# Graph attention over 16 batches: the loads of a batch moved between its four slots, and x in three buffers instead of four

## The chip, the cores and the metric

One core of one Trainium2 chip. The metric is device time in microseconds, the median of several runs; one more execution was recorded by the profiler. The core's engines are TensorE (PE; its weight loads are listed apart as PEld), VectorE (DVE), ScalarE (ACT), GpSimd (POOL) and SyncE (SP). In this kernel SP computes nothing: it issues nearly all DMAs.

## What is computed

A graph attention layer over 16 batches of 512 nodes with 512 features. Each node attends to the first 20 nodes (the "keys"), with 16 heads of 32 features, in two directions (d = 0, 1), each with its own weights and its own view of the adjacency mask. All is 32-bit float. Cut to the core:

```python
row_zero  = v.sum(-1) == 0
q_exp     = where(row_zero[..., None], 0, q[:, None, :])
self_feat = concat([v, q_exp], -1) @ W_self.T + b_self
output    = self_feat
for d in range(2):
    A   = (adj if d == 0 else swapaxes(adj, 1, 2))[:, :, :20, :]     # 11 labels
    kv  = self_feat[:, :20]
    qh, kh = heads(self_feat @ Wq[d].T + bq[d]), heads(kv @ Wk[d].T + bk[d])
    aff = einsum('bnhd,bmhd->bnhm', qh, kh) / sqrt(32)
    aff = where(A.sum(-1) > 0, aff, -9e15) + (A @ w_bias + b_bias)
    w   = softmax(aff, -1)
    output += einsum('bnhf,hgf->bnhg', einsum('bnhm,bmf->bnhf', w, kv), Wout[d]) + bout[d]
return v + relu(output)
```

## The kernel before

Features lie on the partitions (four chunks of 128), nodes along the free dimension. A setup stage (to about 97 us in the profile) makes, for all batches at once, what depends only on the 20 key nodes: the keys already multiplied by the query weights (DRAM buffers `g_d` and `g1_d`), bias scores (`cq_d`), and the values multiplied by the output weights (`vw_d`, later arranged into blocks in `bd_d`). Then a loop runs over the batches b = 0 to 15, and inside it over four tiles `nt` = 0 to 3 of 128 nodes. One pass of the inner loop is called a slot here.

The order is written by hand: `tc.manual_schedule()` keeps each engine's instructions in the order of the program text. What one engine runs is thus fixed, and only semaphores decide when. All loads and stores of the loop are issued by SP, in program order; when one must wait (for its buffer, or for its data), all that stand behind it wait too.

What TensorE does in batch b, in its order:

- slot 0: half of the self features of this batch (`self_feat(b, 0, 1)`, L186, 64 matmuls), then the scores of tile 0 (L250, 128 matmuls);
- slot 1: `self_feat(b, 1, 1)` (64), scores of tile 1 (128);
- slot 2: `attend(b - 1)` (L321: weights times value blocks, for the batch before), scores of tile 2;
- slot 3: the other half of the self features of the next batch (`self_feat(b + 1, 0, 0)` and `(b + 1, 1, 0)`, L186, 128 matmuls), scores of tile 3.

A batch needs these transfers:

| Name | What | Size | First read by |
|---|---|---|---|
| `x` (`load_x`, L88) | node features, features on the partitions | 1024 KB | L186 on TensorE in slot 3 of the batch before; last by `residual` (L335) on GpSimd, in slot 3 of the batch after |
| `xn` (`load_xn`, L92), two halves | the same features, nodes on the partitions | 2 x 512 KB | `row_sum` (L149) on ScalarE, in slot 0 of the batch before |
| `nz` (`load_nz`, L156) | flags of zero rows, written by `row_mask` (L154) in slot 1 | 256 KB | `self_copy` (L199) on VectorE, slot 3 of the batch before |
| `g` (`load_keys`, L110) | keys | 1216 KB | scores (L250) of slot 0 |
| `adj` (`load_adj`, L96), two halves | masks | 2 x 440 KB | `mask_mul` (L207) on ScalarE and `mask_count` (L213) on VectorE: half 0 in slot 2 of the batch before, half 1 in slot 0 |
| `cq` (`load_cq`, L102) | bias scores | 4 x 20 KB | `full_add` (L239) on GpSimd |
| `vd` (`load_values`, L115) | value blocks | 4 x 32 KB | `attend` (L321) in slot 2 of the batch after |
| `out` (`store`, L340) | result of the batch before, four chunks | 4 x 256 KB | stores: two in slot 3, two in the next slot 0, after `residual` (L335) |

In batch 0, `clear_blocks` (L125) zeroes `bd_d` in slot 1, and `blocks` (L142) fills it in slot 2 by 12 DMAs, which wait for the zeroing.

Buffers come from rotating pools: `x` has four, `adj` three, `xn`, `nz`, `cq` and `g` two, `vd` one. A load waits until the last reader of the tile that had its buffer is done. The setup uses one of the x buffers for a weight (`ws_q`). Scores go to PSUM through two buffers (`ps_s`), self features through four (`ps_acc`).

Of the kernel before, what the change touches and what calls it, by code (L numbers as in the profile page):

```python
# [7 lines left out]
F32 = mybir.dt.float32  # L8
# [5 lines left out]
P = 128  # L14
# [4 lines left out]
def gat_kernel(  # L19
# [21 lines left out]
    B, F, N = xT.shape  # L41
    NG, L = adj.shape[3], adj.shape[4]
    H, DH = 16, 32
    C = F // P
# [14 lines left out]
    load = ctx.enter_context(tc.tile_pool(name="load", bufs=2))  # L59
# [24 lines left out]
    xs, xns, rss, adjs, nzs, sfs, cqs, gs, vds = {}, {}, {}, {}, {}, {}, {}, {}, {}  # L84
# [1 line left out]


    def load_x(b):  # L88
        xs[b] = load.tile([P, C, N], F32, tag="x", name=f"x{b}", bufs=4)
        nc.sync.dma_start(xs[b], xT[b].rearrange("(c p) n -> p c n", p=P))  # L90

    def load_xn(b, h):  # L92
        t = xns[b, h] = load.tile([P, 2, F], F32, tag="xn", name=f"xn{b}_{h}")
        nc.sync.dma_start(t, xn[b].rearrange("(p j) f -> p j f", j=4)[:, 2 * h : 2 * h + 2])

    def load_adj(b, h):  # L96
        t = adjs[b, h] = load.tile([P, 2, S * L], I32, tag="adj", name=f"adj{b}_{h}", bufs=3)
        nc.sync.dma_start(
            t, adj[b, h * 2 * P : (h + 1) * 2 * P].rearrange("(t p) d m l -> p t (d m l)", p=P)
        )  # L100

    def load_cq(b):  # L102
        cqs[b] = load.tile([P, HL, S], F32, tag="cq", name=f"cq{b}")
        for a in range(HL):
            nc.sync.dma_start(
                cqs[b][bass.ts(a, R)].rearrange("p h m -> p (h m)"),
                cq_d[b : b + 1, bass.ts(a, HL)].rearrange("b h d m -> b (h d m)").partition_broadcast(R),
            )

    def load_keys(b):  # L110
        gs[b] = gp.tile([P, C, WD], F32, tag="g", name=f"g{b}")
        src = g1_d if b == 1 else g_d[:, :, b - 2]
        nc.sync.dma_start(gs[b].rearrange("p c (a w) -> p (c a) w", a=C), src.rearrange("x p w -> p x w"))

    def load_values(b):  # L115

        vds[b] = gp.tile([P, HL, 2, DH], F32, tag="vd", name=f"vd{b}", bufs=1)
        for c in range(C):
            nc.sync.dma_start(
                vds[b][bass.ts(c, 32)].rearrange("p e i g -> p (e i g)"), bd_d[c, b].rearrange("r e i g -> r (e i g)")  # L120
            )

    def clear_blocks(zero):

        nc.sync.dma_start(  # L125
            bd_d.rearrange("c b r e i g -> (c b r) (e i g)").rearrange("(n p) w -> p n w", p=P),
            zero.unsqueeze(1).to_broadcast([P, C * B * 32 // P, HL * 2 * DH]),
        )

    def blocks():  # L130

        bb = bd_d.rearrange("c b r e i g -> (c b) r e i g")
        vv = vw_d.rearrange("d c (b m) (e g) -> d (c b) m e g", m=NG, e=HL)
        for e in range(HL):
            for i in range(2):
                j = (e * S) // 32 + i
                for d in range(2):
                    lo = max(e * S + d * NG, 32 * j)
                    hi = min(e * S + (d + 1) * NG, 32 * j + 32)
                    if lo < hi:  # L140
                        m, r = lo - e * S - d * NG, lo - 32 * j
                        nc.sync.dma_start(bb[:, r : r + hi - lo, e, i], vv[d, :, m : m + hi - lo, e])  # L142
# [13 lines left out]
    def load_nz(b, queue=nc.sync):  # L156
        nzs[b] = load.tile([P, N], F32, tag="nz", name=f"nz{b}")
        queue.dma_start(nzs[b], nz_d[b : b + 1].partition_broadcast(P))
# [179 lines left out]
    def store():  # L338
        for b, c, o in outs:
            nc.sync.dma_start(out[b, bass.ts(c, P)], o[:, c])  # L340
        outs.clear()


    with tc.tile_pool(name="setup", bufs=1) as sp:
# [12 lines left out]
        ones = sp.tile([P, P], F32, name="ones")  # L357
        br_sb = sp.tile([P, F], F32, name="br_sb")

        ws_q = load.tile([P, C, F], F32, tag="x", name="ws_q", bufs=4)  # L360
        wk_sb = [sfp.tile([P, C, F], F32, tag="sf", name=f"wk{d}") for d in range(2)]

        with tc.tile_pool(name="setup_k", bufs=1) as sk:
# [38 lines left out]
            for d in range(2):  # L402
                rows(wq_sb[:, d], wq[d])
            nc.sync.dma_start(br_sb, b_row.partition_broadcast(P))
            load_x(0)
            nc.sync.dma_start(wb_sb, w_bias.partition_broadcast(P))
            load_adj(0, 0)
# [3 lines left out]
            for d in range(2):  # L411
                rows(wo_sb[:, d], woT[d])
            load_x(1)
            load_adj(0, 1)

# [86 lines left out]
        with tc.tile_pool(name="setup_g", bufs=4) as sg:  # L502
# [116 lines left out]
            for n, runs in enumerate(bursts):  # L619
# [9 lines left out]
                for kind in plan[n - first] if n - first < len(plan) else ():  # L629
                    f, args = steps[kind].pop(0)  # L630
# [25 lines left out]
    with tc.manual_schedule():  # L656
# [11 lines left out]
        for b in range(B):  # L668
# [12 lines left out]
                )  # L681
            for nt in range(NT):
                store()
                if nt == 1:
                    if b + 1 < B:
                        load_adj(b + 1, 0)
                        load_cq(b + 1)
                    if b == 0:
                        clear_blocks(zero)
                if nt == 2:  # L690
                    if b + 1 in rss and b > 0:
                        load_nz(b + 1)
                    if 0 < b < B - 1:
                        load_keys(b + 1)
                    if b == 0:
                        load_adj(1, 1)
                    if b + 2 < B:
                        load_x(b + 2)
                    if 0 < b < B - 1:
                        load_adj(b + 1, 1)  # L700
                    if b + 2 < B:
                        load_xn(b + 2, 0)
                        load_xn(b + 2, 1)
                    if b == 0:
                        blocks()
                if nt == (3 if b + 1 < B else 2):
                    load_values(b)

                if b == B - 1 and nt == 2:
# [85 lines left out]
        b = B - 1  # L795
# [80 lines left out]
```

## Time and profile before

| | |
|---|---|
| Median of 3 runs | 625.6 us (624.79 to 625.65) |
| Profiled execution | 623.73 us, of which the span of the instructions is 621.9 us |
| Granted TensorE clock | 0.995 of full speed |
| DMA traffic | 124.17 MB, mean 200 GB/s; queue q1 (that of SP) 57.5% of the 16 engines' time |
| L250 scores on PE | 285.6 us busy, 8192 matmuls of 293 ns (pipelined) |
| L186 self features on PE | 228.7 us busy, 4096 matmuls of 371 ns (pipelined) |
| PEld waits put down to "issue" | L250 20.6 us (29 times), L186 7.0 us (15 times) |
| DMA issue to landing, median | g 8.7, x 11.0, xn 9.2, adj 7.9, out 3.8, nz 4.4, cq 3.6, vd 5.7 us |

The profile page gives busy time per engine, the queues' traffic, and the chain of work that ended last. Matmuls are pipelined, so the mean of one is longer than the distance between two. "issue" stands for time in which an engine waited for nothing that the profile shows. Besides the page the trace answers questions about stretches of time: the busy time of each engine in a stretch, the DMA engines' share and their rate, and the instructions in order of time, with the idle time before each in square brackets and what ended it. In that timeline a row of SP is the issue of a DMA, not its transfer.

### The profile page before, as it was taken

The page shows a single profiled execution, that of the slowest core. Times are in us where ns is not written, and L with a number is a line of the kernel's source. Part 1 is how long each engine was busy: PE and PEld are TensorE (multiplying, and loading weights), DVE is VectorE, ACT ScalarE, POOL GpSimd, SP SyncE. Part 2 cuts the span into 40 slices and gives each one's busy share as a digit, 9 for nine tenths or more (in the row PEclk, how much of TensorE's full clock was granted, in tenths as well). Part 3 has the DMA queues.
Part 4 walks back from the last instruction along what each step waited for, and adds up shares of the span by engine and source line. Part 5 has one row for each costly group of instructions (what it writes and reads, how often), then busy time and mean ns, then how long its engine had stood idle before and what let it go on. Part 6 is the DMA issues. An engine that isn't in the chain of part 4 may idle for free.

```text
span 621.9 us, 30998 instructions
## 1 busy us (share of the span) xinstructions
PE 607.3 (98%) x13932; PEld 468.4 (75%) x13932; DVE 478.3 (77%) x754; ACT 312.0 (50%) x862; POOL 374.1 (60%) x303
## 2 busy tenths in 40 slices
PE   9999999999999999999999999999999999999995
PEld 6654558787888878878787877878788877787883
DVE  1585657788787878797868788787868797878786
ACT  1334624464555546463637474655546463647561
POOL 3307343557575756666674848475756666675875
PEclk9999999999999999999999999999999999999997
DMA  8999999719282646546381909182735556382503
GB/s 319 385 405 305 356 360 351 181 48 318 60 282 95 223 156 186 192 131 247 93 285 26 332 32 315 56 287 91 243 134 178 201 137 241 79 299 43 167 13 136
DMA packets 97684, 124.17 MB, mean 200 GB/s; under 512 B 19504, under 2 KB 69712, under 8 KB 95504
## 3 DMA queue, kind: packets, MB, share of 16 engines
q1 hardware_dynamic: 96304, 120.31, 57.5%
q8 instruction: 109, 1.79, 1.2%
q0 software_dynamic: 672, 1.36, 1.0%
q10 hardware_dynamic: 576, 0.53, 0.3%
q14 instruction: 23, 0.19, 0.1%
HBM read 82.30 MB, written 40.24 MB: 197 GB/s over the span
## 4 chain that ended last, share of the span: by engine, by line
PE 95%; DVE 3%; issue 1%; ACT 0%; POOL 0%; DVEq 0%; POOLq 0%; ACTq 0%
PE ps_s L250 42%; PE ps_sf L186 35%; PE ps_o L321 5%; PE ps_v L535 3%; PE ps_k L472 3%; PE ps_kv L423 1%; PE ps_warm L382 1%; DVE o L330 0%; PE ps_nz L169 0%; DVE wt L310 0%; DVE ps_s L268 0%; DVE sm L301 0%; DVE full L264 0%; POOL s L303 0%; PE ps_c L508 0%
## 5 line engine op out<-in xcount | busy, mean ns | idle before, releaser
L250 PE MATMUL ps_s<-g,sf 128*32 128x152 f32 x8192 | 285.6, 293 | 4.9 <-issue 4.1
L250 PEld LDWEIGHTS ps_s<-g,sf 128*32 128x32 f32 x8192 | 267.2, 110 | 28.3 <-issue 20.6
L186 PE MATMUL ps_sf<-x,ws_v 128*32 128x236 f32 (+1 forms) x4096 | 228.7, 371 | 1.6 <-issue 1.5
L186 PEld LDWEIGHTS ps_sf<-x,ws_v 128*32 128x32 f32 x4096 | 145.9, 110 | 66.5 <-issue 7.0
L275 ACT ACTIVATE s<-s 128x640 f32<-128x640 f32 x63 | 46.5, 739 | 208.8 <-DVE s L270 206.0
L239 POOL TENSOR_TENSOR full<-cq,both 128x640 f32<-128x640 f32 x64 | 99.9, 1561 | 80.6 <-ACT both L228 61.1
L228 ACT COPY both<-add 32x80 f32<-32x80 f32 x512 | 130.7, 255 | 22.1 <-DVE add L219 16.5
L303 POOL TENSOR_TENSOR s<-s,sm 128x640 f32<-128x640 f32 x63 | 80.3, 1275 | 98.7 <-DVE sm L302 97.6
L264 DVE TENSOR_TENSOR full<-ps_s,full 128x608 f32<-128x608 f32 x63 | 49.6, 787 | 89.4 <-PE ps_s L250 75.3
L335 POOL TENSOR_TENSOR o<-o,x 128x512 f32<-128x512 f32 x60 | 75.9, 1286 | 0.0
L208 POOL TENSOR_TENSOR prod<-prod,wb_sb 128x880 f32<-128x880 f32 x32 | 67.6, 2114 | 8.5 <-ACT prod L207 8.4
L268 DVE TENSOR_REDUCE ps_s<-full 128x32 f32<-128x640 f32 x63 | 52.2, 828 | 2.2
L270 DVE TENSOR_TENSOR s<-full,ps_s 128x640 f32<-128x640 f32 x63 | 51.7, 821 | 2.2
L310 DVE STREAM_TRANSPOSE wt<-s 128x640 f32<-128x640 f32 x63 | 52.8, 838 | 0.1
L301 DVE TENSOR_REDUCE sm<-s 128x32 f32<-128x640 f32 x63 | 51.0, 809 | 1.8
L199 DVE SCALAR_TENSOR_TENSOR sf<-nz,qw,ps_sf 128x236 f32<-128x236 f32 (+1 forms) x128 | 50.0, 441 | 1.2 <-PE ps_sf L186 1.1
L332 ACT ACTIVATE o<-o,bo 128x512 f32<-128x512 f32 x60 | 38.4, 712 | 8.6 <-DVE o L330 8.0
L321 PE MATMUL ps_o<-wt,vd 32*32 32x512 f32 (+2 forms) x1088 | 38.7, 582 | 2.1 <-DVE wt L295 1.9
L330 DVE TENSOR_TENSOR o<-ps_o,sf 128x512 f32<-128x512 f32 x60 | 37.1, 675 | 0.0
L219 DVE TENSOR_REDUCE add<-prod 128x80 f32<-128x960 f32 x32 | 35.6, 1113 | 1.9 <-POOL prod L214 1.9
L149 ACT ACTIVATE xn<-xn 128x512 f32<-128x512 f32 x56 | 34.4, 615 | 0.0
L213 DVE TENSOR_REDUCE cond<-adj 128x80 f32<-128x880 int32 x32 | 32.5, 1014 | 0.0
(213 smaller groups left out, 399.0 us busy)
## 6 DMA issues: line engine op xcount, KB each, us to landing
g<-g_d SPq DMA_DIRECT2D x15, 1216.0 KB, 8.7
g_d<-st SPq DMA_DIRECT2D x16, 1064.0 KB, 5.9
x<-in_xT SPq DMA_DIRECT2D x16, 1024.0 KB, 11.0
out_T<-o SPq DMA_DIRECT2D x60, 256.0 KB, 3.8
xn<-in_xn SPq DMA_DIRECT2D x28, 512.0 KB, 9.2
adj<-in_adj SPq DMA_DIRECT2D x32, 440.0 KB, 7.9
nz<-nz_d SPq DMA_DIRECT2D x14, 256.0 KB, 4.4
wk<-in_wkT SPq DMA_DIRECT2D x2, 1024.0 KB, 7.6
```

What stands on the lines that cost most here:

```text
L186: nc.tensor.matmul(held[0][bass.ts(a, R), i * N // 2 : i * N // 2 + hi - lo], ws_v[:, k, bass.ds((2 * f + i) * P + a * R, R)], xs[b][:, k, ...
L208: nc.gpsimd.tensor_mul(p[:, :, :L], p[:, :, :L], wb_sb.unsqueeze(1).to_broadcast([P, 2 * S, L]))
L228: nc.scalar.copy(adds[b, h][bass.ts(a, R), :, g], add[r].rearrange("p (t m) -> p t m", t=2))
L239: nc.gpsimd.tensor_add(f, cqs[b].unsqueeze(1).to_broadcast(shape), adds[b, nt // 2][:, nt % 2].unsqueeze(2).to_broadcast(shape),)
L250: nc.tensor.matmul(bank[bass.ts(a, R), bass.ts(j, WD // HL)], sfs[b][:, k, bass.ds(nt * P + (2 * g + j) * R, R)], keys[:, k, a], start=(k ...
L268: nc.vector.tensor_reduce(mx, f, AX.X, ALU.max)
L270: nc.vector.tensor_sub(s, f, mx.unsqueeze(3).to_broadcast(full))
L301: nc.vector.tensor_reduce(sm, s, AX.X, ALU.add)
L303: nc.gpsimd.tensor_mul(s, s, sm.unsqueeze(3).to_broadcast(full))
L310: nc.vector.transpose(wts[b][:, nt], s.rearrange("p a h m -> p (a h m)"))
L321: nc.tensor.matmul(banks[a][bass.ts(e, DH)].rearrange("p (t n) -> p t n", n=32), vds[b][r, e, i], wt[r, :, bass.ts(j, 32)], start=start an ...
L335: nc.gpsimd.tensor_add(o[:, c], o[:, c], xs[b][:, c])
```

## The change

The loads change their places in SP's order; the computation stays as it is. In batches 1 to 14, x of the next batch is loaded in slot 0 (before: x of the batch after the next, in slot 2). Slot 1 has the first half of the next batch's masks and `cq`, as before, and now also both halves of `xn` for the batch after the next (before: slot 2). Slot 2 keeps the flags and the keys. The second half of the masks goes from slot 2 to slot 3, ahead of the value blocks; in batch 0 it goes to slot 1. With x fetched later, it has three buffers instead of four.

```diff
     def load_x(b):
-        xs[b] = load.tile([P, C, N], F32, tag="x", name=f"x{b}", bufs=4)
+        xs[b] = load.tile([P, C, N], F32, tag="x", name=f"x{b}", bufs=3)
...
-        ws_q = load.tile([P, C, F], F32, tag="x", name="ws_q", bufs=4)
+        ws_q = load.tile([P, C, F], F32, tag="x", name="ws_q", bufs=3)
...
             for nt in range(NT):
                 store()
+                if nt == 0 and 0 < b < B - 1:
+                    load_x(b + 1)
                 if nt == 1:
                     if b + 1 < B:
                         load_adj(b + 1, 0)
                         load_cq(b + 1)
                     if b == 0:
                         clear_blocks(zero)
-                if nt == 2:
-                    if b + 1 in rss and b > 0:
-                        load_nz(b + 1)
-                    if 0 < b < B - 1:
-                        load_keys(b + 1)
-                    if b == 0:
                         load_adj(1, 1)
-                    if b + 2 < B:
-                        load_x(b + 2)
-                    if 0 < b < B - 1:
-                        load_adj(b + 1, 1)
                     if b + 2 < B:
                         load_xn(b + 2, 0)
                         load_xn(b + 2, 1)
+                if nt == 2:
                     if b == 0:
                         blocks()
+                    if 0 < b < B - 1:
+                        load_nz(b + 1)
+                        load_keys(b + 1)
                 if nt == (3 if b + 1 < B else 2):
+                    if 0 < b < B - 1:
+                        load_adj(b + 1, 1)
                     load_values(b)
```

SP issues 256 DMAs and other rows before and after; for a middle batch their order is now: stores (2), x, first masks, cq (4), xn (2), flag write, nz, keys, stores (2), second masks, value blocks (4).

## The prediction

> **What bounds the kernel now.** I read the page first: the busy shares, the queues, the chain of work that ended last.
>
> ```profile
> PE 607.3 (98%) x13932; PEld 468.4 (75%) x13932; DVE 478.3 (77%) x754; ACT 312.0 (50%) x862; POOL 374.1 (60%) x303
> q8 instruction: 109, 1.79, 1.2%
> PE 95%; DVE 3%; issue 1%; ACT 0%; POOL 0%; DVEq 0%; POOLq 0%; ACTq 0%
> ```
>
> TensorE sets the end; it waits for no load of the loop anywhere. A load can therefore only matter through the last 1%, "issue": TensorE stands still though its data are there. The middle line is a possible reason. The chain runs 13,932 matmuls and as many weight loads; 1.79 MB over these 27,864 instructions is 64 bytes each, and over 109 packets 16.4 KB, or 256 instructions, each. So TensorE's program comes in through the same DMA engines as the data.
>
> Next the stretch view, one batch per row, cut where the scores of slot 2 start (columns: length, then busy time and instructions of PE, PEld, DVE, ACT, POOL, granted clock, DMA share, GB/s).
>
> ```profile
> 300.20:333.94 33.74, 32.78 (x836) 26.95 (x840) 27.11 (x42) 17.95 (x52) 21.62 (x16) 1.00 0.57 175
> 433.57:467.52 33.95, 33.04 (x836) 27.19 (x840) 27.38 (x42) 17.95 (x52) 21.55 (x16) 1.00 0.52 174
> 534.00:566.64 32.64, 32.64 (x836) 26.20 (x840) 27.12 (x42) 18.13 (x52) 21.62 (x16) 1.00 0.55 180
> 566.64:599.36 32.72, 32.72 (x836) 26.41 (x840) 26.94 (x42) 18.10 (x48) 25.16 (x19) 1.00 0.34 100
> ```
>
> The work and the clock are the same in each, the length is not: 32.64 to 33.95 us. From 135.73 to 566.64 lie 13 batches, 430.91 us; 13 x 32.64 = 424.32. So 6.6 us, 0.51 a batch, are lost irregularly. This is nearly all that loads could give back. The last row carries neither x nor its row copy xn (none are left to fetch).
>
> Where a slow batch loses it, by stretches within it and by the weight loads' timeline:
>
> ```profile
> 306.20:310.20 4.00, 4.00 (x88) 2.61 (x82) 3.93 (x6) 0.74 (x1) 3.83 (x4) 1.00 1.06 271
> 314.20:318.20 4.00, 3.65 (x80) 2.38 (x75) 3.02 (x4) 1.57 (x6) 3.00 (x3) 1.00 1.00 296
> 326.20:330.20 4.00, 4.00 (x116) 3.93 (x111) 3.96 (x7) 3.40 (x11) 0.46 (x1) 1.00 0.03 5
> ```
>
> ```profile
> 314.67 1.12 PEld L186 LDWEIGHTS ps_sf<-x,ws_v 128*32 128x32 f32 x24
> 316.62 2.05 PEld L186 LDWEIGHTS ps_sf<-x,ws_v 128*32 128x32 f32 x40 [0.83 <-issue]
> 318.59 2.96 PEld L250 LDWEIGHTS ps_s<-g,sf 128*32 128x32 f32 x87
> 322.47 1.30 PEld L250 LDWEIGHTS ps_s<-g,sf 128*32 128x32 f32 x41 [0.91 <-issue]
> ```
>
> The two gaps break a group in its middle, 128 loads apart (40 + 87, one record short): the length of one instruction packet. The DMA engines are full (share 1.0) from 306 to 318 and idle by 326. The SP timeline names the burst:
>
> ```profile
> 304.06 0.39 SPq L113 DMA_DIRECT2D g<-g_d  x1
> 304.50 5.14 SPq L90 DMA_DIRECT2D x<-in_xT  x1
> 309.73 0.96 SPq L98 DMA_DIRECT2D adj<-in_adj  x1
> 310.79 0.90 SPq L94 DMA_DIRECT2D xn<-in_xn  x2
> 311.78 1.01 SPq L340 DMA_DIRECT2D out_T<-o  x2
> 312.88 5.27 SPq L119 DMA_DIRECT2D vd<-bd_d  x4
> 320.11 1.76 SPq L340 DMA_DIRECT2D out_T<-o  x2
> ```
>
> The trace's packet records put the instruction packets of this batch at 301.27, 308.02, 314.17, 320.19, 325.18, 328.62 us. Counted in weight loads, the first and last come 158 and 167 loads into their packet's turn, the four within the burst 198, 233, 230 and 214. So they are up to 75 loads (2.5 to 3.7 us at 33 to 50 ns) late, and only 128 loads of lead exist: 4.2 us in a scores group (L250), 6.4 in a self-feature pair (L186).
>
> Two rules of the Trainium skill speak against this. "Runtime: NRT & Kernel Launch", Instruction fetch mechanics, has 16 KiB refills overlapping the running page, their cost mostly hidden: then nothing is to be won, and the time stays 625.6. "DMA: Bandwidth & Descriptors", Queues, rings and completion order, has each DMA engine take turns between queues packet by packet, by which a fetch would wait for one packet and not for the burst: again 625.6. The lateness and the gaps above disagree with both, and I follow the rows.
>
> **The change part by part.** No compute instruction changes, nor any byte moved; the SP queue holds the same 256 rows in another order. Times below are those of the batch shown, +33.7 where the next one is meant.
>
> *What it removes.* From slot 2 go x (1024 KB), the second masks (440 KB) and two xn (2 x 512 KB): 2.5 of the 5.8 MB moved in a batch. After nz and keys (some 1.5 MB, 5.5 us at 271 GB/s) the engines come free near 311, when the first rows go out.
>
> *x into slot 0* (about 321, behind the stores at 320.11). It waits for x(b-2)'s buffer. Its last reader, the residual on GpSimd, is what the store just ahead waits for too, so three buffers add no wait. Needed at 338.0 (L186 of the next batch). It landed 11.0 us (median of the DMA list) after issue inside the burst: 332 at the latest, 6 us to spare. Behind it on SP stand first masks and cq, from 322.1 to about 326; the masks are read at 335.0, and they take 3.5 to 8.1 us to land. Cost 0; without the cover, each us of x beyond 338 costs 13 us in all.
>
> *xn into slot 1.* Its buffers are released by ACT's row sums (L149), which end at 329.98, so SP now waits there and issues about 330 to 331. Behind it in the queue is only the flag write at 335.89, which waits for VectorE anyway. Cost 0; a flag write late by 1 us would delay nz, keys and sf, which have 2 to 6 us.
>
> *Second masks into slot 3*, the tight one: behind the stores, issued at 312.9, ahead of the value blocks (not read for 19 us). Readers are ACT's cast at 318.36 (ACT idles 7.5 us after it) and VectorE's count at 319.61 (idle 2.79 us before L264). Landing after 3.5 us gives 316.4, in time; after 8.1 us 321.0, so VectorE is 1.4 us late, inside its idle time. TensorE next needs that scores bank at 333.9. Bounds: 0 and, absorbed, 0; I take 0.
>
> *SP's own waits*: it stood 30.8 us in all for x and 26.9 for xn before it could issue value blocks and stores. These go, and nothing that TensorE reads was behind them: 0.
>
> *Batches 0 and 1*: x(2) is issued after blocks() at about 127 instead of 102, needed near 140. Batch 0 has one gap of 1.08 us at 109.41 under the zeroing and masks, which stay; bounds 0 and -1.1, I take 0.
>
> *Instruction packets*: the clusters are now about 5.5 us (nz, keys), 4 us (stores 0.5 MB, masks 0.44, value blocks 0.13), 7 us (stores, x, masks, cq: 2.0 MB at 296 GB/s) and 3 us (xn). The 7 us one begins near 320, with 2 us of scores, then 3.45 us of L186 pairs: a packet asked for there has over 5 us of lead. What stays per batch is bounded by 0 (row 534.00) and 1.31 (row 433.57). The nearest row is 566.64:599.36, where keys, masks, stores and value blocks ran without x and xn: 0.08. I add 0.04 for x's cluster (an estimate): 0.12 x 13 = 1.6.
>
> **Sum.** 1.6 - 6.6 = -5.0 us. The profiled execution took 623.73 (span 621.9 and 1.8 around it), so 618.7; it lies 1.9 below the runs' median of 625.6, so the median should be 620.6.
>
> **Rivals.**
> *The stalls only move (no change).* For: the bytes and the mean DMA share (0.55) stay, so as many packets meet some traffic. Against: the lead covers a short wait, and row 566.64 shows it. 0.5 a batch again: 625.6.
> *Slower, by packets caught under scores.* Slot 0's cluster runs on into slot 1's scores, whose lead is only 4.2 us; if each batch met that as 433.57:467.52 did, the excess is 1.31 instead of 0.51: +0.8 x 13 = +10.4, 636. It decides from an excess of 0.6 (1.25 us in all). For: in the batch shown the second gap, 0.91, is in slot 0's scores. Against: there the burst was in its fifteenth microsecond.
> *Slower, by late masks.* VectorE has 32.7 - 27.1 = 5.6 us idle a batch; masks landing over 12.3 us after issue (319.61 + 5.6 - 312.9) would use it up, and each us beyond costs 13. The DMA list has 7.9 as median: unlikely.
> *The change doesn't do what it says* is excluded by the order of the SP rows.
>
> **How the numbers follow.** A measurement here tells 0.2% (1.25 us) from nothing. Forecast 0.72 (all of it faster); stalls move 0.13 (same); packets under scores 0.11 and late masks 0.04 (slower). The forecast's own range runs from 617.5 (all 6.6 gone, batch 0's 1.1, 0.4 of scatter) to 624.0. To leave out no more than 0.2 the top goes over the no-change case, to 626.5.
>
> **What would show it.** Right: batches of 32.6 to 32.9 us; "issue" before L250 and L186 weight loads (20.6 and 7.0 us, of which 0.84 before each slot-2 group stays) falling by most of the irregular part; DMA share in four humps; instruction packets no more than some 50 loads late. Wrong: gaps of 0.5 to 1 us in slots 0 and 1; TensorE waiting for "DMA x"; VectorE's L213 waiting for adj with idle time before L264 gone; batches above 33.2 us.

## The result, and the profile after

The changed kernel takes 616.93 us (median of 4 runs, 615.88 to 620.02); the kernel before, in runs beside it, 625.19. The ratio is 0.9878, with a 95% interval of 0.9838 to 0.9918: 7.6 us less by the ratio, 8.3 by the medians. It became faster, as forecast (620.6), by more than forecast (-5.0). The median ends 0.6 us below the low end of the range (617.5); the ratio lies just inside it (617.5 / 625.6 = 0.9870). The profiled execution took 616.01 us, its span is 614.2 us: 7.7 below the 621.9 of before.

The page of the changed kernel: busy time, the chain that ended last, and the weight loads of the two large groups (group, busy time and mean, idle time of the engine before them and what ended most of it).

```profile
PE 602.9 (98%) x13932; PEld 470.4 (77%) x13932; DVE 477.3 (78%) x754; ACT 311.9 (51%) x862; POOL 373.4 (61%) x303
PE 95%; DVE 3%; issue 1%; ACT 0%; POOL 0%; DVEq 0%; POOLq 0%; ACTq 0%
L250 PEld LDWEIGHTS ps_s<-g,sf 128*32 128x32 f32 x8192 | 265.3, 110 | 22.3 <-issue 14.8
L186 PEld LDWEIGHTS ps_sf<-x,ws_v 128*32 128x32 f32 x4096 | 147.0, 110 | 61.1 <-issue 3.3
```

TensorE still sets the end. What shrank are the two "issue" figures: 20.6 to 14.8 and 7.0 to 3.3 us, together 9.5. Of what is left, 15 x 0.84 = 12.6 us are the gap before the scores of each slot 2, in both kernels.

The stretch view, cut at the scores of slot 2 as for the kernel before:

```profile
137.22:169.45 32.23, 32.23 (x841) 25.62 (x833) 25.55 (x40) 16.70 (x49) 20.46 (x16) 1.00 0.58 183
428.35:461.77 33.42, 32.61 (x837) 28.88 (x832) 27.36 (x42) 17.97 (x53) 21.57 (x16) 1.00 0.57 177
559.33:591.56 32.23, 32.23 (x835) 25.61 (x832) 26.45 (x42) 17.95 (x47) 24.82 (x19) 1.00 0.36 102
```

Six of the 14 batches take 32.23 or 32.24 us, below the best batch of before (32.64). One still takes 33.42. The prediction's sign of being right was batches of 32.6 to 32.9 us: two fit it and eleven are shorter. The one of 33.42 is over the 33.2 that it named as a sign of being wrong. The 14 batches from the first such cut to the last need 454.35 us instead of 463.63: -9.3. Against that, the stretch from the first scores to the first cut (batches 0 and 1) grew from 45.12 to 46.23 us, +1.1, and the setup ended 0.4 later. The end after the last cut is the same (22.64 and 22.66). Sum: -7.7.

Inside a batch (the one from 298.78 to 331.37 us) the DMA share, last but one in each row, now comes in humps:

```profile
304.78:308.78 4.00, 4.00 (x88) 4.00 (x82) 3.93 (x6) 0.74 (x1) 3.84 (x4) 1.00 0.97 259
312.78:316.78 4.00, 4.00 (x94) 3.98 (x87) 2.62 (x4) 1.11 (x5) 3.08 (x3) 1.00 0.39 138
316.78:320.78 4.00, 4.00 (x128) 3.95 (x123) 3.45 (x6) 1.47 (x2) 2.93 (x3) 1.00 0.67 216
320.78:324.78 4.00, 4.00 (x92) 3.99 (x84) 3.03 (x4) 0.50 (x1) 3.50 (x3) 1.00 0.87 310
324.78:328.78 4.00, 4.00 (x130) 3.84 (x122) 2.97 (x6) 3.94 (x15) 1.27 (x1) 1.00 0.35 110
```

The stretch 14 to 18 us into the batch had the share 1.00 and lost 0.35 us of PE time before; now it has 0.39 and PE is busy throughout. SP's timeline of the same batch names the humps:

```profile
303.54 0.39 SPq L113 DMA_DIRECT2D g<-g_d  x1
309.06 1.58 SPq L340 DMA_DIRECT2D out_T<-o  x2
310.69 0.81 SPq L98 DMA_DIRECT2D adj<-in_adj  x1
311.59 1.83 SPq L119 DMA_DIRECT2D vd<-bd_d  x4
316.52 1.60 SPq L340 DMA_DIRECT2D out_T<-o  x2
318.18 0.43 SPq L90 DMA_DIRECT2D x<-in_xT  x1
318.65 0.55 SPq L98 DMA_DIRECT2D adj<-in_adj  x1
319.25 2.25 SPq L105 DMA_DIRECT2D cq<-cq_d  x4
326.27 1.70 SPq L94 DMA_DIRECT2D xn<-in_xn  x2
```

Issuing x takes 0.43 us instead of 5.14, the value blocks 1.83 instead of 5.27. The DMA share while x is issued is now 0.67; before it rose to 1.06 meanwhile. "Slots" are places in a program, not times: x, masks and cq go out at once, and only xn is held back, by ScalarE's row sums.

### The profile page after: what moved, and what is told of

It reads as the page before. It is cut to its first block, busy times and chain, and to the rows that moved or that the text cites. A ratio compares the mean times of both kernels' runs of the same rounds, so it can differ in the third digit from the quotient of the medians.

```text
span 614.2 us, 31034 instructions
## 1 busy us (share of the span) xinstructions
PE 602.9 (98%) x13932; PEld 470.4 (77%) x13932; DVE 477.3 (78%) x754; ACT 311.9 (51%) x862; POOL 373.4 (61%) x303
## 2 busy tenths in 40 slices
DMA packets 97684, 124.17 MB, mean 202 GB/s; under 512 B 19504, under 2 KB 69712, under 8 KB 95504
## 4 chain that ended last, share of the span: by engine, by line
PE 95%; DVE 3%; issue 1%; ACT 0%; POOL 0%; DVEq 0%; POOLq 0%; ACTq 0%
PE ps_s L250 42%; PE ps_sf L186 35%; PE ps_o L321 6%; PE ps_v L535 3%; PE ps_k L472 3%; PE ps_kv L423 2%; PE ps_warm L382 1%; DVE o L330 0%; PE ps_nz L169 0%; DVE wt L310 0%; DVE ps_s L268 0%; DVE sm L301 0%; DVE full L264 0%; POOL s L303 0%; PE ps_c L508 0%
## 5 line engine op out<-in xcount | busy, mean ns | idle before, releaser
L250 PEld LDWEIGHTS ps_s<-g,sf 128*32 128x32 f32 x8192 | 265.3, 110 | 22.3 <-issue 14.8
L250 PE MATMUL ps_s<-g,sf 128*32 128x152 f32 x8192 | 280.0, 293 | 1.6 <-issue 1.0
L186 PE MATMUL ps_sf<-x,ws_v 128*32 128x236 f32 (+1 forms) x4096 | 224.3, 371 | 0.6 <-issue 0.6
L186 PEld LDWEIGHTS ps_sf<-x,ws_v 128*32 128x32 f32 x4096 | 147.0, 110 | 61.1 <-issue 3.3
L239 POOL TENSOR_TENSOR full<-cq,both 128x640 f32<-128x640 f32 x64 | 99.9, 1561 | 80.6 <-ACT both L228 64.9
```

Of the source, the lines that this page charges most:

```text
L186: nc.tensor.matmul(held[0][bass.ts(a, R), i * N // 2 : i * N // 2 + hi - lo], ws_v[:, k, bass.ds((2 * f + i) * P + a * R, R)], xs[b][:, k, ...
L239: nc.gpsimd.tensor_add(f, cqs[b].unsqueeze(1).to_broadcast(shape), adds[b, nt // 2][:, nt % 2].unsqueeze(2).to_broadcast(shape),)
L250: nc.tensor.matmul(bank[bass.ts(a, R), bass.ts(j, WD // HL)], sfs[b][:, k, bass.ds(nt * P + (2 * g + j) * R, R)], keys[:, k, a], start=(k ...
```

## The experiments

Ratios are to the kernel before, run beside each. Theory A: TensorE's instruction packets come late because of the loads. Theory B: data and stores come earlier. Theory C: writes into SBUF slow TensorE. The "loop loss" is the 14 batches' time over 14 x 32.23 = 451.2 us, in one profiled execution.

### Unread traffic in one place: extra_sbuf, extra_dram

```diff
                     load_values(b)
+                    if 0 < b < B - 2:
+                        for i in range(2):
+                            extra = work.tile([P, C, N], F32, tag=f"extra{i}", name=f"extra{b}_{i}", bufs=1)
+                            nc.sync.dma_start(extra, xT[b + i].rearrange("(c p) n -> p c n", p=P))
```

In extra_dram the target is a DRAM tile.

> The changed kernel with two more loads of 1024 KB (x tiles again, into tiles that nothing reads) after the value blocks in slot 3 of batches 1 to 13: 13 x 2 MB. No reader, so nothing waits for them. Theory A (TensorE's instruction packets queue behind loads): the burst over slots 3 and 0 is back, batches go from 32.2 to 33 or more, and the time from 616.9 to 624 to 632. Theory B (the gain came from data and stores arriving earlier, since SP no longer stands for x and xn): x, first masks and cq land some 5 us later but still in time, so 617 to 619. Theory C (writes into SBUF slow TensorE's reads): slower too, with longer matmuls and no gaps put down to issue.

> The same two extra transfers, from DRAM to DRAM, so that nothing is written into SBUF. Theory A: as slow as with SBUF targets, 624 to 632, with gaps of 0.2 to 1.2 us in the middle of L186 and L250 groups. Theory B: 617 to 619. Theory C: 617 to 619, as no SBUF write is added.

Measured: 635.3 us, ratio 1.0156 (1.0106 to 1.0206), and 636.9 us, 1.0195 (1.0139 to 1.0251); loop loss 22.5 and 20.7 us. Both are over the 632 expected. What TensorE waited for in extra_sbuf (sum, times, longest), the two longest rows:

```profile
PE ps_sf L186 <- issue: 7.4, 6, 2.2
PE ps_s L250 <- issue: 4.8, 5, 2.4
```

And the weight loads of one batch of extra_dram:

```profile
427.31 0.54 PEld L186 LDWEIGHTS ps_sf<-x,ws_v 128*32 128x32 f32 x9
430.18 2.52 PEld L186 LDWEIGHTS ps_sf<-x,ws_v 128*32 128x32 f32 x51 [2.33 <-issue]
432.60 0.31 PEld L250 LDWEIGHTS ps_s<-g,sf 128*32 128x32 f32 x2
432.80 0.12 PEld L186 LDWEIGHTS ps_sf<-x,ws_v 128*32 128x32 f32 x2
432.82 2.60 PEld L250 LDWEIGHTS ps_s<-g,sf 128*32 128x32 f32 x73
436.32 1.70 PEld L250 LDWEIGHTS ps_s<-g,sf 128*32 128x32 f32 x53 [0.90 <-issue]
```

Data that nobody reads cost 18 to 20 us against the changed kernel, and TensorE shows no wait for a load of the loop: B falls as the main cause. With no byte more into SBUF the cost is about the same: C falls. Between the two gaps lie 51 + 2 + 2 + 73 = 128 loads.

Not all of the cost is standing. Right after the three longest gaps of the weight loads (2.68 and 2.66 us in extra_sbuf, 2.83 in extra_dram) the granted clock, third column from the end, falls to half for 3.4 us; the first row is of extra_sbuf, the second of extra_dram:

```profile
499.20:502.60 3.40, 3.40 (x36) 1.65 (x32) 2.12 (x4) 3.37 (x13) 1.10 (x1) 0.51 0.87 297
566.60:570.00 3.40, 3.40 (x40) 2.97 (x33) 3.33 (x5) 0.99 (x2) 0.00 (x0) 0.50 0.51 182
```

By an estimate (half of 3.4 us each time) this makes 3.4 of the 22.5 us and 1.7 of the 20.7. After shorter gaps, up to 2.33 us in these two, the clock stayed at full, and the loops of the other executions have no such fall.

### One part of the change alone: x_only, xn_only, x_and_xn

x_only and xn_only are the kernel before with that load moved as in the change; x_and_xn is the changed kernel with

```diff
                         load_keys(b + 1)
+                        load_adj(b + 1, 1)
...
-                    if 0 < b < B - 1:
-                        load_adj(b + 1, 1)
                     load_values(b)
```

> The kernel before with only x moved to slot 0 (three buffers). Theory A: the burst of slot 2 shrinks from some 20 to 16 us but x's MB falls into slot 0 right after it, so less than half of the 8.3 us: 621 to 624. Theory B: SP's 30.8 us of standing for x go, and with them most of the loss: 617 to 619.

> The kernel before with only xn moved to slot 1. Theory A: 1 MB leaves the burst for a stretch in which the DMA engines were idle (326 to 338 us in the profile before), so about half of the gain: 619 to 622. Theory B: SP's 26.9 us of standing for xn at the stores go: 619 to 622, not told apart by the time, but by the instruction packets' lateness.

> The changed kernel with the second masks back in slot 2, behind the keys: x and xn are moved, the masks are not. x alone gave nothing (626.2 against 625.5), xn alone 2 us. Theory A (packets queue behind the length of a cluster): slot 2's cluster grows from 1.5 to 1.9 MB, from 5.5 to 7 us, still short; 616 to 619. If the masks in slot 3 are what counts: 623 or more.

| Kernel | us | Ratio (95%) | Loop loss, us |
|---|---|---|---|
| x_only | 626.2 | 1.0022 (0.9988 to 1.0056) | 13.3 |
| xn_only | 623.8 | 0.9967 (0.9937 to 0.9996) | 11.3 |
| x_and_xn | 618.1 | 0.9877 (0.9848 to 0.9907) | 8.2 |

(The profiled execution of x_and_xn, 620.9 us of span, was one of its longer ones.) Both single moves stayed behind what A expected: x alone gains nothing, xn alone some 2 us, both together more than 7. B is contradicted by x_only: SP's wait for x before the value blocks (30.8 us before) is gone, and the time stays. A batch of x_only, weight loads:

```profile
279.42 2.91 PEld L250 LDWEIGHTS ps_s<-g,sf 128*32 128x32 f32 x88
283.01 1.27 PEld L250 LDWEIGHTS ps_s<-g,sf 128*32 128x32 f32 x40 [0.69 <-issue]
284.20 3.36 PEld L186 LDWEIGHTS ps_sf<-x,ws_v 128*32 128x32 f32 x64
287.57 0.86 PEld L250 LDWEIGHTS ps_s<-g,sf 128*32 128x32 f32 x23
289.12 3.37 PEld L250 LDWEIGHTS ps_s<-g,sf 128*32 128x32 f32 x105 [0.70 <-issue]
292.38 1.12 PEld L186 LDWEIGHTS ps_sf<-x,ws_v 128*32 128x32 f32 x23
295.32 2.08 PEld L186 LDWEIGHTS ps_sf<-x,ws_v 128*32 128x32 f32 x41 [1.82 <-issue]
```

Three packets in a row are late (40 + 64 + 23 = 127 and 105 + 23 = 128 loads apart), the third in slot 1. The stretch view of the same batch (DMA share last but one):

```profile
277.08:281.08 4.00, 4.00 (x104) 3.10 (x100) 3.93 (x7) 2.01 (x6) 3.74 (x4) 1.00 1.03 293
281.08:285.08 4.00, 3.62 (x106) 3.29 (x100) 1.53 (x5) 3.07 (x13) 2.10 (x2) 1.00 1.05 384
285.08:289.08 4.00, 3.65 (x79) 3.25 (x71) 3.78 (x6) 1.56 (x2) 3.12 (x3) 1.00 0.68 249
289.08:293.08 4.00, 3.95 (x117) 3.88 (x121) 2.07 (x5) 0.00 (x0) 3.57 (x3) 1.00 0.94 297
293.08:297.08 4.00, 2.66 (x53) 1.46 (x46) 3.93 (x5) 1.57 (x4) 1.87 (x2) 1.00 0.51 180
```

xn still fills slot 2's burst, and x follows right behind it in slot 0: the traffic lasts some 20 us, as it did before, where A had expected 16. The second masks' move isn't told apart from nothing (618.1 against 617.2 in runs beside each other, intervals overlapping).

### The changed kernel again, and finer cuts: after_again, x2_early, finer, finer_again, xn_late

x2_early loads x(2) in slot 2 of batch 0 (four buffers). finer, where `load_x_half` loads two of x's four chunks:

```diff
                 if nt == 0 and 0 < b < B - 1:
-                    load_x(b + 1)
+                    load_x_half(b + 1, 0)
...
                     if b + 2 < B:
                         load_xn(b + 2, 0)
-                        load_xn(b + 2, 1)
+                    if 0 < b < B - 1:
+                        load_x_half(b + 1, 1)
...
                     load_values(b)
+                if nt == 3 and b + 2 < B:
+                    load_xn(b + 2, 1)
```

xn_late leaves x whole, puts the first half of xn behind the keys in slot 2 and the second as in finer.

> The changed kernel once more, on the same chip as the three beside it: 616 to 618 by every theory. How far its batches spread around 32.23 us shows how much of the difference between executions lies in when instruction packets come.

> The changed kernel with x(2) loaded in slot 2 of batch 0 as before (four buffers). Between the first scores and batch 1's third slot the changed kernel lost 1.5 us against before, with a gap of 1.5 us at 136 us behind x(2) and two xn. Theory A: that gap goes, 615 to 616. If it stays, x(2) isn't its cause: 617.

> Loads cut finer: x in two halves, the second behind the first half of xn, which ScalarE's row sums hold back to about 328 us; the second half of xn in slot 3 behind the value blocks. Clusters of 1.5, 1.0, 1.5 and 1.6 MB instead of 2.0, 1.0, 1.5 and 1.1. Theory A: no cluster lasts over 5.5 us, so fewer late packets; 612 to 616. If only the largest burst mattered, no more is to be had: 616 to 618. If x's second half is late, TensorE waits for DMA x: over 620.

> The finer cut once more, for the size of its difference to the changed kernel (616.3 against 617.2 us, within the scatter): 615 to 617 if it is a little better, 617 or more if that was scatter.

> The changed kernel with the first half of xn behind the keys in slot 2 and the second behind the value blocks in slot 3: nothing is under way around attend, but the clusters of slots 2, 3 and 0 (2.0, 1.6, 2.0 MB) nearly touch. Theory A: gaps at 0 to 3 us go, gaps at 13 to 22 us come back; 616 to 622, no better than the changed kernel.

| Kernel | us | Ratio (95%) | Loop loss, us |
|---|---|---|---|
| after_again | 617.2 | 0.9865 (0.9840 to 0.9890) | 6.9 |
| x2_early | 619.4 | 0.9887 (0.9862 to 0.9912) | 7.3 |
| finer | 616.3 | 0.9833 (0.9812 to 0.9854) | 4.9 |
| finer_again | 614.7 | 0.9835 (0.9815 to 0.9855) | 2.4 |
| xn_late | 618.0 | 0.9893 (0.9874 to 0.9912) | 5.6 |

The two executions of the changed kernel lost 3.1 and 6.9 us in the loop: the same program, with other packets late. In x2_early the gap at 136 us is gone, but from the first scores to the first cut it needs 45.7 us, where the changed kernel had 46.2 and 45.9; the time isn't better, and the expected 615 to 616 was a miss. finer is the best version run, twice at 0.983 to 0.984; its interval and that of after_again, run beside it, overlap by a hair, so the 0.3% over the changed kernel is likely, not proven. In xn_late no gap lies in the 3 us after the cut, and gaps 12 to 19 us into a batch are back, as expected (others stay at 27 to 29 us); it is no better.

### Less traffic, and traffic spread: no_xn, extra_spread

```diff
-                    if b + 2 < B:
-                        load_xn(b + 2, 0)
-                        load_xn(b + 2, 1)
+                    if b == 0:
+                        load_xn(2, 0)
+                        load_xn(2, 1)
+                    elif b + 2 < B:
+                        xns[b + 2, 0], xns[b + 2, 1] = xns[2, 0], xns[2, 1]
```

This is no_xn. extra_spread adds, to the changed kernel, one 512 KB load at the end of the load block of each slot.

> The changed kernel without the loads of xn after the first: the row sums of batches 3 to 15 are taken from batch 2's rows, so 13 MB less are moved. Theory A: the gaps around attend and the scores of slot 2 (28 to 32 us and 0 to 3 us into a batch), where only xn is under way, go; 612 to 615. If those gaps have another cause, 616 to 618.

> The changed kernel with the same 2 MB a batch of unread loads into SBUF, but in four pieces of 512 KB, one in each slot, instead of both in slot 3 (635.3 us). If the sum of the traffic sets the loss, 632 to 638 again. Theory A, where the unbroken length of a cluster counts: 620 to 628.

no_xn: 615.9 us, 0.9856 (0.9832 to 0.9880), loop loss 2.6 us. In its execution no gap lies in the 3 us after a cut, where xn passes in the changed kernel; those at 13 and 28 us remain, so only half of the expectation came true: xn isn't the only cause of the gaps at 28 us. The time lies just over the range and isn't told apart from the changed kernel's.

extra_spread: 632.3 us, 1.0097 (1.0063 to 1.0131), where theory A expected 620 to 628: a miss, and inside the 632 to 638 of the rival, by which the sum of the traffic sets the loss. Spreading the 2 MB took off at most about a fifth of its cost (1.0156 for one place, against 0.987 without it; the two intervals overlap). That fifth is 3.7 us, about what the half-clock stretches made in the profiled execution of extra_sbuf (3.4), so it isn't shown that fewer packets came late. Each of the four humps is half a megabyte longer here, so the length of the longest run isn't all that counts. The sum isn't all either: the kernels before and after move the same 124.17 MB.

## Why the prediction was right in kind and off in size

**The mechanism is shown in its main part.** In the 14 profiled executions 107 gaps of the weight loads put down to "issue" and over 0.45 us lie between the first and the last cut (the regular 0.84 before slot 2's scores left out). By the trace's packet records they end 2.2 to 2.8 us after the latest instruction packet of TensorE began to move (median 2.4; two after 3.3 and 3.7). The regular gaps show no such tie: they end 0.0 to 6.6 us after one. The gaps stand at fixed places of the program. Counted in weight loads recorded before them, the same places come back in different kernels: 5556 (x_only, xn_only, xn_late), 5811 (extra_sbuf, extra_dram, x_only), 6449 (x_only, xn_only, xn_late), 7597 (extra_sbuf, after_again, xn_late), 9765 (x_only, xn_only, x_and_xn). Their distances are multiples of 127.5 to 127.6 loads. Only which of these boundaries hurts, and by how much, changes with the DMA order. A late load would hold a group at its first matmul instead. So a late packet stops TensorE, and the traffic sets which packets are late.

Why a packet starts late is argued, not shown. Once it moves it is no slower than the others (median 0.99 us against 1.04), so it is the start that is late; but no record tells when it was asked for, nor where it waited. The two rules that the prediction quotes from the Trainium skill gave 625.6; the measured 616.9 and the cost of unread traffic speak against that use of them as far as this kernel goes. Late packets also remain: counted as in the prediction, 21 of 91 in the loop were over 50 loads late before, 10 of 94 after; the sign "no more than some 50 loads late" was not met.

**The mis-sized term** is the sum's first: "So 6.6 us, 0.51 a batch, are lost irregularly. This is nearly all that loads could give back." It measured each batch against the best of before, 32.64 us, as if that one lost nothing. It lost 0.41 too: the changed kernel's undisturbed batches take 32.23, and so does the quickest batch of 12 of the 14 executions. So the loop had 463.63 - 451.22 = 12.4 us to give, not 6.6. The profile held this: the weight loads' "issue" time in L250 and L186, 27.6 us, less 15 x 0.84 = 12.6, leaves 15.0 (1.3 of it in batch 0). The prediction kept these rows for its last part instead of setting them against its floor. A loss of this size hardly shows as a gap: against a batch of 32.23 us, the chain of the batch of 32.64 fell behind by 0.13 us in the scores of slot 0 and by 0.29 from slot 1's self features to attend, and no listed gap of the weight loads there is over 0.18.

**What stays** was put at 1.6 us, by the one batch without x and xn: measured 3.1 and 6.9 in two executions. That batch was no clean neighbour: its 0.08 was counted from the same wrong floor and is 0.49. 14 x 0.49 = 6.9 would have lain nearer to the mean of the two, 5.0; that it equals one of them is chance.

**Batches 0 and 1** were put at 0, with bounds of 0 and -1.1; they lost 1.1. The bound left out a loss: x(2) and xn behind it now pass just before attend, and TensorE stands 1.47 us there for one packet (with x(2) earlier, in x2_early, that gap is missing). 12.4 - 3.1 = 9.3 gained, 1.1 lost here and 0.4 in the setup make the 7.7 of the profiled pair. That the forecast was off by only 2.7 there is partly luck: the floor hid 5.8 us of gain, and the other three took 3.0 back.

**The zeros held.** Three x buffers add no wait: x goes out right behind the stores (318.18 after 316.52) and lands after 5.2 us, at 323.4; L186 reads it from 335.7. SP waited 59.7 us in all for ScalarE's row sums before xn, and TensorE shows no wait for what stands behind it. The second masks, issued at 310.69, land after 4.1 us, at 314.8, and no wait of ScalarE or VectorE for masks is listed (GpSimd's L239 has 11.4 us, before 15.2). The count of 256 rows for SP doesn't agree with the trace, where SP issues 387 DMAs in each kernel, setup included; that the number stays the same holds.

**The rivals.** "The stalls only move" is what x alone does (ratio 1.0022). "Packets caught under scores" is what remains of the loss: at the start of the batch of 33.42 us, the scores of slot 2 stopped after 9 loads. The packet that ended this began to move at 427.38, in attend, with xn under way (DMA share 0.80 from 424 to 426):

```profile
426.97 0.55 PEld L321 LDWEIGHTS ps_o<-wt,vd 32*32 32x32 f32 x31 [0.32 <-issue]
428.36 0.27 PEld L250 LDWEIGHTS ps_s<-g,sf 128*32 128x32 f32 x9 [0.84 <-issue]
429.75 2.35 PEld L250 LDWEIGHTS ps_s<-g,sf 128*32 128x32 f32 x76 [1.12 <-issue]
```

The prediction looked for it in slots 0 and 1. In the changed kernel's two executions all eight gaps over 0.45 us are some 28 to 29 us into the batch (slot 1's scores) or in the first 3 us of the next. Late masks didn't occur.

## What to carry to other kernels

Where TensorE is busy 98% and no load is late, the order of the loads can still be worth 1%: its program comes through the same DMA engines, and a packet of 256 instructions that comes late in heavy traffic stops it in the middle of a group. Look for gaps put down to "issue", a fixed count of instructions apart, and break up the long runs of transfers as a whole: moving one load may only attach it to the next, and traffic added in small pieces still cost most of what it cost in one place. When a loss is read off as "over the best batch", check the floor against an independent row, here the summed "issue" time.

## What the runs showed that was not expected

- 2 MB a batch of transfers that nothing reads or waits for cost 18 to 20 us over 13 batches, 1.4 to 1.5 us each, about the same into SBUF (packets of 2 KB) and from DRAM to DRAM (packets of 64 KB).
- Less transfer time per load came with the spreading: x lands after 6.1 us instead of 11.0 (median), xn after 4.7 instead of 9.2, at the same bytes.
- One program's executions differ by 4 us (615.9 to 620.1 for the changed kernel); of the two that were profiled, 4.1 us apart, 3.7 us of the difference lay in the loop.
- Three gaps of 2.66 to 2.83 us were each followed by 3.4 us at half the granted clock; no gap of 2.33 us or less inside the loop was.
